# A grouped 3x3 convolution with a residual: where the input waits for its sum, and where the products are added

## The chip, the cores and the metric

The kernel runs on one core of one Trainium2 chip. The metric is the device time of one execution in microseconds. The three runs of the kernel before took 999.61, 989.73 and 990.78 us, median 990.78. The profile is of a further execution, which has its own time.

In what follows PE is the matrix engine, PEld its weight loads, DVE the vector engine, ACT the scalar engine, POOL the general engine (GpSimd), and SP the engine that issues most of the transfers. L494 is line 494 of the kernel before. Where a helper records the operation, its line is shown.

## What is computed

Input x is 160 images of 128 channels by 32 x 32, in float32 (512 KB an image). U holds five sets of weights for a 3x3 convolution from 128 to 128 channels. Image 5b + n uses set n.

```python
s1 = (max(U) - min(U)) / 3;  v1 = s1 * floor(U / s1)
s2 = s1 / 5;                 v2 = s2 * floor((U - v1) / s2)
w = v1 + v2                               # the weights, quantised twice
g = groupnorm(x, 32 groups, eps=1e-5)     # 4 channels x 1024 points a group
out = x + conv3x3(g, w[set of the image], padding 1)
```

So each output image is the input image plus a product: the input is needed twice, to be normalised and to be added.

## The kernel before

**Order of the work.** `Main.run` walks the images set by set: image i is number i % 32 of set i // 32. The order on every engine is the order in which this program issues instructions; it is written by hand (a manual schedule), and every engine and every transfer queue takes its instructions in that order. One iteration of the loop issues the matmuls of image i and, for other images, what must run beside them: PE products of i + 1 (`sums_of_pairs`), DVE low part of i + 2, ACT high part of i + 3, POOL and DVE combinations of i + 4 (L674, L704 on POOL; L686, L693 on DVE), and the statistics of images up to 14 ahead (`STAT_LEAD`), which on ACT are L241 and L248. Three of five images are "combined": differences and sums of neighbouring columns are taken on the image before it is normalised, which needs fewer matmuls (L839) than the other images do (L784 as well). For other images POOL normalises (L710).

**Input buffers.** Images are loaded in pairs ("chunks", 1 MB) by SP, L494, into one of 12 buffers named xt. A load is issued when the loop is within `LOAD_LEAD` = 20 images of the chunk (chunks 0 to 5 before the loop, so chunk 6 is images 12 and 13). The tile framework makes it wait until what was in the buffer has been used and stored.

**Leaving PSUM.** An image's product is finished in a pair of PSUM banks (eo). In the next iteration `residual` copies it on ACT to one of 3 sum buffers (L922), and `accumulate` lets POOL issue a transfer that adds the sum buffer onto the image in its xt buffer, in SBUF (L945, 512 KB). Fifteen images are added "by hand", by DVE, from PSUM onto the image (L937, L939, L929): the first three, the last four (`LAST`), and every sixteenth (i % 16 == 7) after image 30.

**Stores.** At the end of iteration i `store(i - 2)` lets SP store a whole chunk, L950, if i - 2 is its second image. The last four images are stored singly (L941, L932). The store waits for both accumulations.

**SP's queue.** Loads, stores and the weights' loads (L487, one per set, for sets 1 to 4 in the loop: at iteration 2, and for set n + 2 at the last but one image of set n) stand in one queue. Each iteration ends with these two steps:

```python
            while loaded * NB < min(self.imgs, i + self.LOAD_LEAD):
                self.load(loaded)
                loaded += 1
            self.store(i - 2)
```

**Weights.** A set's quantisation is a list of single steps (`Later`), taken a few per iteration on DVE, with some on ACT (L134). It begins at image 1 of the set before (at image 4 for set 1); its first step is ACT's L134, which reads the loaded weights (tile u).

Of the kernel before, what the change touches and what calls it, by code (L numbers as in the profile page):

```python
# [11 lines left out]
ALU = mybir.AluOpType  # L12
# [9 lines left out]
NB = 2  # L22
LAST = 4
# [13 lines left out]
class Later:  # L37


    def __init__(self, steps=(), pace=0.0):  # L40
        self.steps = iter(steps)
        self.pace, self.due = pace, 0.0
        self.scalar = False
# [19 lines left out]
    def finish(self):  # L63
        run(self.steps)
# [256 lines left out]
def general_path(tc, keep, steps, x, u, out):  # L321
# [8 lines left out]
    with tc.If(far > 0), ExitStack() as ctx:  # L330
# [9 lines left out]
        for n in range(N_SETS):  # L340
            un = one.tile([P, C, TAPS], F32, tag="u", name=f"g_u{n}")
            nc.sync.dma_start(un, uv[n])
            wn = one.tile([P, C, TAPS], F32, tag="w", name=f"g_w{n}")
            k1, k2 = run(steps.quantise(one, un, f"g{n}", F32))
            nc.vector.tensor_scalar_mul(wn, k1, steps.s1)
            nc.vector.scalar_tensor_tensor(wn, k2, steps.s2, wn, ALU.mult, ALU.add)
# [38 lines left out]
class Main:  # L385
# [22 lines left out]


    STAT_LEAD = 14  # L410
    LOAD_LEAD = 20
    STEADY = 7
    BY_VECTOR = (8, 10, 11, 14, 19, 24, 29, 34)
    FIFTHS = 30
# [10 lines left out]
    def __init__(self, tc, ctx, keep, x, u, out):  # L425
        self.tc = tc
        nc = self.nc = tc.nc
        self.imgs, C, self.H, self.W = x.shape
        P = self.P = nc.NUM_PARTITIONS
        assert C == P and self.H * self.W == 1024  # L430
        self.per_set = self.imgs // N_SETS
        self.xv = x.rearrange("(b n) c h w -> n c b (h w)", n=N_SETS)
        self.ov = out.rearrange("(b n) c h w -> n c b (h w)", n=N_SETS)
        self.uv = u.rearrange("n (o i k) -> n o i k", o=C, k=TAPS)

        def pool(name, bufs, **kw):
            return ctx.enter_context(tc.tile_pool(name=name, bufs=bufs, **kw))

        self.const = pool("const", 1)
        self.qpool = pool("quant", 1)  # L440
        self.wpool = pool("weights", 2)
        self.upool = pool("u", 1)
        self.xpool = pool("x", 12)
        self.zpool = pool("z", 2)
        self.parts = pool("parts", 4)
        self.rows = pool("rows", 4)
        self.wide = pool("wide", 2)
        self.wide_parts = pool("wide_parts", 3)
        self.evac = pool("evac", 2)
        self.sums = pool("sums", 3)  # L450
        self.unread = pool("unread", 1)
        self.small = pool("small", 3)
        self.ps_eo = pool("ps_eo", 2, space=PSUM)
        ps_m = pool("ps_m", 1, space=PSUM)
        ps_small = pool("ps_small", 1, space=PSUM)
        self.steps = Steps(nc, keep)

        self.m1a, self.m1b, self.m2_ps = (
            ps_m.tile([P, self.H // 2, self.W], F32, tag=name, name=name)
            for name in ("m1a", "m1b", "m2")  # L460
        )
        self.pair = [self.m1a, self.m2_ps]

        small = ps_small.tile([P, 512], F32, tag="small", name="small")
        self.pt, self.pg = small[:, : ROW * P].rearrange("p (k o) -> p k o", k=ROW), small[:, ROW * P :]
        self.chunks, self.z, self.hi, self.v, self.eo, self.m2 = {}, {}, {}, {}, {}, {}
        self.sum = {}
        self.tables, self.wts, self.across = {}, {}, {}
        self.columns = []

        cuts = [0, 2, 4, 8, 12, 16, 20, *range(24, self.imgs + 1, 8)]
        self.groups = [range(a, b) for a, b in zip(cuts, cuts[1:])]
        self.group_of = {i: k for k, g in enumerate(self.groups) for i in g}
        self.stats = {}
# [117 lines left out]
    def keep_sums(self, n, col):  # L592
        wt = self.wts[n, col]
        run(self.both_sums(
            self.nc.gpsimd, wt[:, self.SUM], wt[:, self.DIFF], *(wt[:, k] for k in range(ROW))
        ))
# [317 lines left out]
    def residual(self, i):  # L914

        nc = self.nc
        eo = self.eo.pop(i)
        del self.hi[i]
        n, b = self.place(i)
        if not self.by_hand(i):  # L920
            self.sum[i] = self.sums.tile([self.P, 1024], F32, tag="sum", name=f"sum{i}")
            nc.scalar.copy(self.as_banks(i, self.sum[i]), self.flat(i, eo))  # L922
            return
        xj = self.image(i)
        if i == self.imgs - 1:
            image, banks = self.as_banks(i, xj), self.flat(i, eo)
            for a, quarters in ((0, (slice(0, 512),)), (1, (slice(0, 256), slice(256, 512)))):
                for h, q in enumerate(quarters):
                    nc.vector.tensor_add(image[:, a, q], banks[:, a, q], image[:, a, q])  # L929
                    if a == 1:  # L930
                        half = slice(h * 512, h * 512 + 512)
                        nc.sync.dma_start(self.ov[n, :, b, half], xj[:, half])  # L932
            return
        image = self.as_banks(i, xj)
        if eo is self.pair:
            for a in range(2):
                nc.vector.tensor_add(image[:, a], self.bank(eo, a), image[:, a])  # L937
        else:
            nc.vector.tensor_add(image, self.flat(i, eo), image)  # L939
        if i >= self.imgs - LAST:  # L940
            nc.sync.dma_start(self.ov[n, :, b], xj)  # L941

    def accumulate(self, i):
        if i in self.sum:
            self.nc.gpsimd.dma_start(self.image(i), self.sum.pop(i), accum_op=ALU.add)  # L945

    def store(self, i):
        if 0 <= i < self.imgs - LAST and i % NB == NB - 1:
            n, b = self.place(i)
            self.nc.sync.dma_start(  # L950
                self.ov[n, :, b - NB + 1 : b + 1, :], self.chunks[i // NB]
            )

    def run(self):
        nc, P = self.nc, self.P
# [125 lines left out]
        run(self.combinations(3))  # L1081
        self.steps.choose()
        ready, middle, scaled, measured, loaded = [], [], [], self.EARLY, 6
        later, turned = Later(), []
        for i in range(self.imgs):
            n, b = self.place(i)
# [135 lines left out]
            for k in to_measure:  # L1222
                group = self.group_of[k]
                if k + 1 == self.groups[group].stop:
                    ready.append(self.stats[group])
            while loaded * NB < min(self.imgs, i + self.LOAD_LEAD):
                self.load(loaded)
                loaded += 1
            self.store(i - 2)
        self.residual(self.imgs - 1)  # L1230


# [46 lines left out]
```

## Time and profile before

| | |
|---|---|
| median of 3 runs | 990.78 us (989.73 to 999.61) |
| the profiled execution: its time | 1001.85 us |
| the profiled execution: span in the trace | 1000.1 us |
| mean granted PE clock | 0.988 |
| moved by transfers | 250.05 MB, 250 GB/s |
| read from HBM, written to HBM | 89.19 MB, 83.89 MB |
| loads of a chunk (78 x 1024 KB) | median 7.3 us from issue to landing |
| stores of a chunk (78 x 1024 KB) | median 11.1 us |
| accumulations (145 x 512 KB) | median 8.1 us |

How to read it: a busy time is the sum over the engine's instructions; a line such as "ACT junk L241 <- DMA xt<-in_x_dram: 28.7, 15, 7.6" says that ACT stood idle before the instructions of L241 that write junk, until transfers from the input into xt had landed, for 28.7 us in all, 15 times, 7.6 us at the longest. The waits of SP's queue (SPq) are told apart from those of the computing engines, since a queue may stand without anything being late. In the DMA lines q1 is the queue of SP's transfers, q0 that of POOL's; packets, MB, and the time of the packets as a share of 16 transfer engines. Of the packets those under 512 bytes (5136 in all) are completions; a data packet of an image is 4096 bytes, one row of one partition, so an image is 128 packets, 8 on each engine.

### The profile page before, as it was taken

Reading aid. Unit: us, or ns where it says so; the run is one execution under the profiler, and the core shown is the slowest. Engines: PE = TensorE matmul, PEld = TensorE weight load, DVE = VectorE, ACT = ScalarE, POOL = GpSimd, SP = SyncE. Lnnn points to the kernel's source line nnn. Section 1 sums busy time; section 2 is a strip of 40 time slices with the busy share of each in tenths; the row PEclk is TensorE's granted clock in tenths of the full one; section 3 lists DMA queues with packets and bytes.
Section 4 is the critical chain, followed back from the end, with each engine's and each line's share of the span. In section 5 each row is a group of like instructions: output and inputs, shape, how many; then the busy total and the mean of one; then the engine's idle time right before and its main releaser. Section 6 shows DMA issues by size and latency. Waiting matters only on the chain. (4 is left out here: it accounts for less than half of the span.)

```text
span 1000.1 us, 13146 instructions
## 1 busy us (share of the span) xinstructions
PE 937.4 (94%) x4444; PEld 435.7 (44%) x4444; DVE 917.8 (92%) x1290; ACT 851.9 (85%) x1160; POOL 455.7 (46%) x466
## 2 busy tenths in 40 slices
PE   2999999999999999969999999799999999999996
PEld 1444444444444444424444444344444444444443
DVE  7999999999999999959999999599999978889995
ACT  5789998999999998859889999689988979888551
POOL 4354346445434444514354436244444555555640
PEclk9999999999999999979999999899999999999999
DMA  9738899999999998999999989998999999999765
GB/s 361 285 106 234 222 254 249 250 259 283 264 244 257 258 270 240 258 251 273 280 250 261 259 213 263 285 249 225 285 237 259 276 250 251 243 258 301 179 168 190
DMA packets 66268, 250.05 MB, mean 250 GB/s; under 512 B 5136, under 2 KB 5136, under 8 KB 66192
## 3 DMA queue, kind: packets, MB, share of 16 engines
q1 hardware_dynamic: 45312, 173.09, 51.6%
q0 software_dynamic: 20880, 76.03, 39.2%
q8 instruction: 37, 0.61, 0.2%
q14 instruction: 39, 0.32, 0.1%
HBM read 89.19 MB, written 83.89 MB: 173 GB/s over the span
## 5 line engine op out<-in xcount | busy, mean ns | idle before, releaser
L784 PE MATMUL eo<-hi,wt 128*128 128x496 f16 (+3 forms) x1206 | 319.9, 375 | 1.5 <-ACT wt L566 0.9
L839 PEld LDWEIGHTS <-wt 128*128 128x128 f16 x1884 | 183.9, 99 | 225.2 <-DVE rows L769 12.6
L740 DVE SCALAR_TENSOR_TENSOR vl<-v,rstd,vh 128x2048 f16<-128x2048 f32 x92 | 218.7, 2377 | 2.3 <-ACT vh L734 2.2
L839 PE MATMUL eo<-vh,wt 128*128 128x512 f16 x552 | 207.8, 377 | 0.5 <-DVE eo L898 0.4
L839 PE MATMUL eo<-vl,wt 128*128 128x512 f16 x552 | 207.5, 376 | 0.0
L734 ACT ACTIVATE vh<-v,rstd 128x2048 f16<-128x2048 f32 x92 | 184.1, 2001 | 20.3 <-DVE v L693 20.0
L674 POOL TENSOR_SCALAR v<-xt,ngm 128x64 f32<-128x64 f32 x92 | 79.5, 864 | 238.7 <-issue 100.3
L784 PEld LDWEIGHTS <-wt 128*128 128x128 f16 x1278 | 124.2, 99 | 145.7 <-DVE eo L898 4.0
L241 ACT ACTIVATE junk<-xt 128x1024 uint8<-128x1024 f32 x152 | 160.5, 1056 | 31.5 <-DMA xt<-in_x_dram 28.7
L839 PEld LDWEIGHTS <-across 128*128 128x128 f16 x1104 | 108.7, 98 | 152.6 <-issue 31.1
L248 ACT ACTIVATE junk<-xt,mv 128x1024 uint8<-128x1024 f32 x152 | 174.4, 1147 | 0.1
L922 ACT COPY sum<-eo 128x1024 f32<-128x1024 f32 x145 | 151.6, 1046 | 23.4 <-PE eo L839 21.9
L710 POOL TENSOR_SCALAR z<-xt,ngm,rstd 128x1024 f32<-128x1024 f32 x50 | 89.9, 1798 | 174.4 <-DVE rows L768 63.1
L839 PE MATMUL eo<-rows,wt 128*128 128x496 f16 (+1 forms) x390 | 148.1, 380 | 0.0
L945 POOL DMA_DIRECT2D xt<-sum x145 | 126.8, 874 | 17.8 <-ACT sum L922 15.0
L839 PE MATMUL m<-vh,across 128*128 128x496 f16 (+1 forms) x276 | 104.8, 380 | 11.7 <-ACT m L887 11.7
L839 PE MATMUL m<-vl,across 128*128 128x496 f16 (+1 forms) x276 | 104.8, 380 | 10.2 <-DVE vl L740 10.1
L887 ACT ACTIVATE m<-m 128x512 f32<-128x512 f32 x157 | 93.8, 597 | 20.6 <-PE m L839 16.6
L686 DVE TENSOR_TENSOR v<-xt 128x960 f32<-128x960 f32 x92 | 106.6, 1159 | 0.0
L704 POOL TENSOR_TENSOR v<-xt 128x512 f32<-128x512 f32 x92 | 97.3, 1057 | 0.0
L747 DVE TENSOR_TENSOR lo<-z,hi 128x1024 f16<-128x1024 f32 x68 | 83.1, 1222 | 0.0
L896 DVE SCALAR_TENSOR_TENSOR eo<-m1b,m 128x512 f32<-128x512 f32 x79 | 54.9, 695 | 18.7 <-ACT m L887 16.1
(146 smaller groups left out, 1182.4 us busy)
## 6 DMA issues: line engine op xcount, KB each, us to landing
xt<-in_x_dram SPq DMA_DIRECT2D x78, 1024.0 KB, 7.3
out_dram<-xt SPq DMA_DIRECT2D x78, 1024.0 KB, 11.1
xt<-sum POOLq DMA_DIRECT2D x145, 512.0 KB, 8.1
u<-in_L_conv_U_dram SPq DMA_DIRECT2D x4, 576.0 KB, 14.3
xt<-in_x_dram SPq DMA_DIRECT2D x4, 512.0 KB, 9.6
range<-in_L_conv_U_dram SPq DMA_DIRECT2D x3, 576.0 KB, 7.7
out_dram<-xt SPq DMA_DIRECT2D x3, 512.0 KB, 2.7
u<-in_L_conv_U_dram SPq DMA_DIRECT2D x2, 288.0 KB, 3.1
```

Of the source, the lines that this page charges most:

```text
L241: self.nc.scalar.activation(junk, image, ACTF.Copy, scale=-1.0 / image.shape[1], accum_out=self.mv[:, j, 0:1],)
L248: self.nc.scalar.activation(junk, image, ACTF.Square, bias=self.mv[:, j, 0:1], accum_out=self.mv[:, j, 1:2],)
L686: nc.vector.tensor_tensor(self.view(v, 1, (511, 2), (half, H), (1, half - 1)), self.view(x, 1, (1, 2), (W, H), (2, half - 1)), self.view(x ...
L704: ins = nc.gpsimd.tensor_sub(self.v[i][:, 1536:], odd, even)
L710: ins = nc.gpsimd.tensor_scalar(z, self.image(i), st.ngm[:, j], st.rstd[:, j], ALU.add, ALU.mult)
L734: self.nc.scalar.mul(vh, self.v[i], st.rstd[:, j])
L740: yield self.nc.vector.scalar_tensor_tensor(vl, self.v[i], st.rstd[:, j], self.hi[i], ALU.mult, ALU.subtract)
L784: nc.tensor.matmul(self.bank(target, a)[:, first:end, c0:c1], self.wts[n, col][:, k, :], tile[:, s0 : s0 + 2 * (end - first) - 1 : 2, c0 + ...
L839: self.nc.tensor.matmul(out, weights, moving, start=start and j == 0, stop=False, skip_group_check=True)
L887: self.nc.scalar.mul(m2, self.m2_ps, 0.5)
L922: nc.scalar.copy(self.as_banks(i, self.sum[i]), self.flat(i, eo))
L945: self.nc.gpsimd.dma_start(self.image(i), self.sum.pop(i), accum_op=ALU.add)
```

## The change

A chunk is stored to the output unchanged, as soon as it has been loaded: it is put on a list when its load is issued, and taken from the list, one per iteration, four iterations later or after (`store_input`). The product of an image is then added onto the output in DRAM, not onto the image in SBUF, by the same kind of transfer from POOL; it waits for the store of the image's input (`self.stored`). Images that are added by hand are stored singly, after DVE has added the product, and their chunk's other image is then stored singly too. A load into a used buffer is no longer issued by a fixed lead but when its chunk's images have been read (`consumed`): at image i - 2, or, for an image that is added by hand, at i + 2. `LOAD_LEAD`, 18, governs the first 12 chunks alone. Image 2, the first that is added by hand, is now stored from `residual` at once. Line numbers after L411 move: by 1 at first, by 17 to 23 from `accumulate` on.

```diff
-    LOAD_LEAD = 20
+    LOAD_LEAD = 18
+    CHUNKS = 12
...
-        if i >= self.imgs - LAST:
-            nc.sync.dma_start(self.ov[n, :, b], xj)
+        self.store(i)
 
     def accumulate(self, i):
+
         if i in self.sum:
-            self.nc.gpsimd.dma_start(self.image(i), self.sum.pop(i), accum_op=ALU.add)
+            n, b = self.place(i)
+            added = self.nc.gpsimd.dma_start(
+                self.ov[n, :, b], self.sum.pop(i), accum_op=ALU.add
+            )
+            self.after(added, self.stored[i].ins)
 
     def store(self, i):
-        if 0 <= i < self.imgs - LAST and i % NB == NB - 1:
-            n, b = self.place(i)
-            self.nc.sync.dma_start(
-                self.ov[n, :, b - NB + 1 : b + 1, :], self.chunks[i // NB]
-            )
+
+        n, b = self.place(i)
+        return self.nc.sync.dma_start(self.ov[n, :, b], self.image(i))
+
+    def store_input(self, c):
+
+        images = [i for i in range(c * NB, c * NB + NB) if not self.by_hand(i)]
+        if len(images) == NB:
+            n, b = self.place(images[0])
+            stored = self.nc.sync.dma_start(self.ov[n, :, b : b + NB, :], self.chunks[c])
+            self.stored.update((i, stored) for i in images)
+            return
+        self.stored.update((i, self.store(i)) for i in images)
+
+    def consumed(self, c):
+
+        return max(i + 2 if self.by_hand(i) else i - 2 for i in range(c * NB, c * NB + NB))
...
         ready, middle, scaled, measured, loaded = [], [], [], self.EARLY, 6
+        due = [(c, c) for c in range(1, loaded)]
...
-            while loaded * NB < min(self.imgs, i + self.LOAD_LEAD):
+            while loaded * NB < self.imgs and (
+                loaded * NB < i + self.LOAD_LEAD if loaded < self.CHUNKS
+                else i >= self.consumed(loaded - self.CHUNKS)
+            ):
                 self.load(loaded)
+                due.append((i + 4, loaded))
                 loaded += 1
-            self.store(i - 2)
+            if due and due[0][0] <= i:
+                self.store_input(due.pop(0)[1])
         self.residual(self.imgs - 1)
```

More of the change, by code (lines that the diff above doesn't have):

```diff
@@ L442, in __init__ @@
         self.upool = pool("u", 1)
-        self.xpool = pool("x", 12)
+        self.xpool = pool("x", self.CHUNKS)
         self.zpool = pool("z", 2)
@@ L466, in __init__ @@
         self.chunks, self.z, self.hi, self.v, self.eo, self.m2 = {}, {}, {}, {}, {}, {}
-        self.sum = {}
+        self.sum, self.stored = {}, {}
         self.tables, self.wts, self.across = {}, {}, {}
```

## The prediction, made before the changed kernel had run

> **What bounds the kernel now.** I read the page first (engines, slices, queues), then the waits of all engines and of SP's queue, the timelines of SP and ACT around the largest stall, the windows of 25 us, and the DMA view of two windows. The page:
>
> ```profile
> span 1000.1 us, 13146 instructions
> PE 937.4 (94%) x4444; PEld 435.7 (44%) x4444; DVE 917.8 (92%) x1290; ACT 851.9 (85%) x1160; POOL 455.7 (46%) x466
> DMA  9738899999999998999999989998999999999765
> q1 hardware_dynamic: 45312, 173.09, 51.6%
> q0 software_dynamic: 20880, 76.03, 39.2%
> ```
>
> Three things are nearly full at once: PE, DVE, and the 16 DMA engines, at 51.6 + 39.2 = 91% over the span and 9 tenths in nearly every slice. q1 holds loads and stores, q0 the accumulating transfers: 44% of q1's bytes in 76% of its time. The waits, of ACT, then of SP's queue:
>
> ```profile
> ACT junk L241 <- DMA xt<-in_x_dram: 28.7, 15, 7.6
> ACT nnn L134 <- DMA u<-in_L_conv_U_dram: 21.0, 2, 12.0
> ```
>
> ```profile
> SPq L494 <- DMA out_dram<-xt: 702.4, 67, 14.9
> SPq L950 <- DMA xt<-sum: 109.1, 16, 16.1
> ```
>
> SP spends 702 us inside a load's wait: the buffer is free only when the store of its last content has left, and that store waits for two accumulations. While SP stands, all behind it stands. Two timelines show what it costs, SP's and then ACT's:
>
> ```profile
> 411.89 0.42 SPq L950 DMA_DIRECT2D out_dram<-xt  x1
> 425.62 0.37 SPq L494 DMA_DIRECT2D xt<-in_x_dram  x1
> 426.08 0.44 SPq L950 DMA_DIRECT2D out_dram<-xt  x1
> 426.61 0.42 SPq L487 DMA_DIRECT2D u<-in_L_conv_U_dram  x1
> ```
>
> ```profile
> 440.97 0.80 ACT L134 ACTIVATE nnn<-u,s1r 128x384 int16<-128x384 f32 x1 [12.03 <-DMA u<-in_L_conv_U_dram]
> ```
>
> The weights' load stood behind a load that stood behind a store for 13.7 us; it went out at 426.61, ACT wanted it at 428.9 and got it at 440.97. The windows price this and the late stretch (columns: width, PE, PEld, DVE, ACT, POOL busy, clock, DMA share, GB/s):
>
> ```profile
> 400.00:425.00 25.00, 24.75 (x118) 11.34 (x116) 23.15 (x29) 21.90 (x29) 13.95 (x13) 1.00 1.00 257
> 425.00:450.00 25.00, 15.85 (x64) 6.87 (x63) 13.76 (x21) 12.94 (x20) 3.33 (x4) 0.80 0.89 251
> 450.00:475.00 25.00, 25.00 (x121) 11.60 (x121) 24.42 (x35) 24.57 (x34) 11.91 (x13) 1.00 0.99 274
> 625.00:650.00 25.00, 19.78 (x88) 8.82 (x86) 14.94 (x26) 16.29 (x24) 6.97 (x8) 0.86 0.97 284
> 800.00:825.00 25.00, 23.03 (x110) 10.70 (x109) 19.25 (x19) 19.98 (x27) 13.26 (x12) 1.00 0.95 250
> ```
>
> Elsewhere PE and DVE are both at 24 to 25 of 25. From 787 to 898 the chain that ended last is a row of stores, one behind the other. The DMA view of 8 to 24 us (loads alone), then of 100 to 420 us:
>
> ```profile
> q1 hardware_dynamic: 1723, 6.59, 102.3%
> ```
>
> ```profile
> q1 hardware_dynamic: 13897, 53.64, 51.3%
> q0 software_dynamic: 7544, 27.50, 44.2%
> ```
>
> A packet of 4096 bytes costs an engine 1.023 x 16 x 16 us / 1576 = 166 ns where loads are alone (1723 less 147 small ones); in the mix a copy costs 0.513 x 16 x 320 / 13096 = 200 ns and an accumulation 0.442 x 16 x 320 / 6714 = 337 ns, about twice an unhindered copy: it reads two operands.
>
> **The change, part by part.**
>
> *Store early, load without the store's wait.* A chunk's store now needs only its load, so the 702 and 109 us of SP's waiting go. A load into a used buffer still waits for its old store, but that was issued long before (from chunk 21 on, four iterations after its load), and for the engines' last reads. It goes out at iteration 2c-1 for images 2c+24 and 2c+25, 25 images ahead, where it was at most 20. Its first reader comes 14 images ahead, so some 11 iterations of slack stand where there were 6 less SP's delay. The mean pace is (974.9 - 69.8) / 152 = 5.95 us per image, from the first and last accumulation (images 3 to 155). By-hand images (every 16th) hold their chunk 4 iterations longer; their loads keep 7, or 41 us.
>
> What goes: (a) the weights' waits, 12.0 + 8.9 = 20.9 us. The other two such loads were not waited for. The load is now issued some 4 iterations (23 us) before its reader; the median landing was 14.3. (b) From 800 to 925 us PE idles 5.6 us in five windows, with 1.8 us of half clock: 7. ACT's other waits on loads outside that stretch lie beside a busy DVE: 0. Behind the stalls the next limit is late at once: DVE at 24.5 of 25 in sets 0 to 3, PE after that. Sum: 28 us. All of PE's idle time between 75 and 975 us (33) and the lost clock (10: half speed for about 20 us) bound it from above: 43; from below 0, if the DMA engines, not SP, are what is late (second case below).
>
> *The front of SP's queue.* Image 2's store, which did not exist as a separate one, now stands ahead of the loads of images 12 to 17 and waits for DVE's L937, which ended at 54.04. Those loads went out between 15 and 24 us; now at about 54.5. Image 12 lands after 0.5 + 1 MB at 412 GB/s (6.59 MB in 16 us) plus 2 us, at 60; ACT read it at 59.4 and stood 2.3 us for PE at 62.9: 0. Behind it are 3 loads, 2 half stores, a load and set 1's weights: 6.1 MB, 15 us, so 72 against ACT's 72.4: between 0 and 4, I take 1.
>
> *Stores of the first 20 chunks.* They go out one per iteration, twice the pace, when the DMA slices at 50 to 125 us have 0.17 to 0.65 of their time free; backlog is covered by the 11 iterations. More issues by SP: 14, about 0.4 us each, on a queue that is now idle: 0.
>
> *POOL's wait for the early store.* Chunk 5's store is the tightest: behind 5 MB of burst loads from 86 us, at about 228 GB/s beside accumulations, it lands at 112 and image 10 adds at about 122. 0. If it is late, what stands behind on POOL is z or the outer columns of the image 4 ahead, then DVE's L686.
>
> *The accumulation itself.* Count, bytes and POOL's issue (869 ns) stay; the second operand and the result move to DRAM. No row shows such a transfer. From below, the present 337 ns: a load (read from HBM) and a copy in the other direction share one queue and one price. From above 2 x 200 = 400 ns, two mixed copies; with the issues' medians of 11.1 us for a store against 7.3 for a load, 337 x 1.5 = 505 at the extreme. I take 337, the row of the same operation. If landings grow, ACT's L922 waits: three sum buffers give some 16 us, and the median landing is 8.1, the longest 12.1.
>
> The Trainium skill, DMA: Bandwidth & Descriptors, Anatomy of one DMA, speaks against this: the receipt of the last write dominates a transfer's fixed 2 us, and is longest when the target is HBM. By that each accumulation lands later; with 3 buffers it changes nothing in the sum unless the delay passes about 8 us. HBM Reference, Specifications, gives 358 GB/s as a core's share; HBM traffic after is 173 + 2 x 76 = 325 MB, 908 us by that and 789 us by the 412 GB/s read here, so neither binds.
>
> *Sum.* The profiled execution took 1001.85 us: 1001.85 - 28 + 1 = 975. The median of the runs, 990.78, is 11 lower. If those runs simply had less of these stalls, 975 stands; if they were quicker throughout, 964. I take 970.
>
> **Rivals.**
>
> *The DMA engines stay the limit (no change).* From the landing of the last load (about 906) to the end took 94 us before, and must again. Until that load q1 must move, from 54 us on, 148 loads and 156 stores of 8 packets per engine, q0 129 accumulations (to about image 138), and 8 us of weights: at mixed prices 304 x 8 x 0.200 + 129 x 8 x 0.337 + 8 = 842 us. 54 + 842 + 94 = 990, about the median. For it: shares of 0.99 in the windows. Against: at the unhindered 166 ns it is 54 + 759 + 94 = 907, and nothing binds; the DMA now has a full queue where it had SP's gaps.
>
> *Accumulating in DRAM costs more (slower).* Place: q0, all images. Each 10 ns more is 129 x 8 x 0.010 = 10 us once the engines are full. At 400 ns: 990 + 65 = 1055. It decides (1% slower than 1001.85, 1012) from 358 ns at mixed copy prices, from 440 at unhindered ones. For it: DMA has no room; reads of HBM come between writes of HBM. Against: read and write copies cost alike here, and the accumulation's price is just that of two reads.
>
> *A new stall at the front only.* Set 1's weights or image 12 late, 4 to 8 us: 975 to 980. It does not decide the sign.
>
> **How the numbers follow.** About 1% is what a measurement can tell from no change. Stalls gone: 0.50, front stall included, 970, own range 957 to 981. DMA still the limit: 0.17, 981 to 1001. Dearer accumulation: 0.33, 1001 to some 1100, half of it below 1035. So faster 0.50, same 0.17, slower 0.33. Low 955: most of the 43 us bound. High 1035: beyond it lie 0.16 of the third case, and little below 955.
>
> **What would show it.** SP's wait of L494 for out_dram falls from 702 us to under 100; ACT's L134 no longer waits for u; window 425:450 has PE at 24 or more; stores move ahead, and DMA slices after 900 us fall to 5 tenths. The price step is right if q0's share stays near 39% of the span (337 ns each); over 42% at an unchanged span it is wrong, and ACT's L922 or L241 would wait for DMA. I am wrong if PE's idle time grows in windows where DMA is at 1.0.

## The result, and the profile after

The kernel after took 986.12 us (median of 20 runs, 984.95 to 987.55). Beside it the kernel before took 999.0 (20 runs, 985.46 to 1009.21); the ratio is 0.9917, interval 0.9892 to 0.9941, faster by 0.8%. (The ratio leaves out the runs of the kernel before that lie over 1.5% above its fastest, so it is nearer to 1 than the two medians are.) The forecast was 970, range 955 to 1035: the sign held and the time lies inside the range, but the gain is 0.8% where 2.1% was forecast (970 against 990.78). The profiled execution took 985.5 us, against 1001.85 before: 16 us less where the sum said 27. From the page after (written to HBM is higher by 76.02 MB, the accumulations, which wrote to SBUF before):

```profile
span 983.8 us, 13047 instructions
PE 931.5 (95%) x4444; PEld 434.3 (44%) x4444; DVE 915.7 (93%) x1290; ACT 853.2 (87%) x1160; POOL 457.8 (47%) x466
DMA  9079999999989997999799989989997999766653
q1 hardware_dynamic: 45472, 173.09, 45.9%
q0 software_dynamic: 20880, 76.03, 42.6%
HBM read 89.19 MB, written 159.91 MB: 253 GB/s over the span
```

The waits of ACT, then of SP's queue:

```profile
ACT nnn L134 <- DMA u<-in_L_conv_U_dram: 13.2, 2, 11.9
ACT junk L241 <- DMA xt<-in_x_dram: 10.3, 3, 7.6
```

```profile
SPq L955 <- DVE xt L940: 327.1, 12, 90.1
SPq L495 <- DVE v L694: 147.9, 16, 12.7
SPq L962 <- DMA xt<-in_x_dram: 110.7, 21, 11.1
SPq L495 <- POOL z L711: 102.8, 14, 11.2
...
SPq L495 <- DMA out_dram<-xt: 23.6, 11, 6.3
```

SP's loads wait 24 us for old stores, where it was 702. SP's queue is not idle for that: all rows of this view add up to 794 us, against 903 before. It now stands for DVE to finish images that are added by hand (L955), for the last reads of a buffer (L495), and for loads to land (L962). ACT's wait for loaded images fell from 28.7 to 10.3 us, of which 9.4 stand before 60 us in both kernels. One long wait for weights is left, 11.9 us, and it is not one of the two that stood before: it belongs to set 2. The timelines of SP and of ACT show it:

```profile
222.83 0.53 SPq L495 DMA_DIRECT2D xt<-in_x_dram  x1
233.22 0.37 SPq L962 DMA_DIRECT2D out_dram<-xt  x1
233.64 1.05 SPq L488 DMA_DIRECT2D u<-in_L_conv_U_dram  x1
```

```profile
256.66 0.80 ACT L134 ACTIVATE nnn<-u,s1r 128x384 int16<-128x384 f32 x1 [11.94 <-DMA u<-in_L_conv_U_dram]
```

SP stood from 223 to 233 at an early store (L962), which waits until the chunk that it stores, issued at 203.71, has landed; the weights' load was behind it. It went out at 233.64, ACT wanted it at 244.72, and it was used at 256.66. The windows (columns as before: width, PE, PEld, DVE, ACT, POOL busy, clock, DMA share, GB/s):

```profile
225.00:250.00 25.00, 25.00 (x120) 11.52 (x118) 20.23 (x22) 19.53 (x26) 13.66 (x11) 1.00 1.05 305
250.00:275.00 25.00, 17.19 (x77) 7.72 (x76) 16.80 (x29) 18.28 (x26) 8.52 (x9) 0.86 1.03 372
...
425.00:450.00 25.00, 25.00 (x122) 11.89 (x121) 22.52 (x33) 23.84 (x33) 11.32 (x11) 1.00 1.04 330
...
625.00:650.00 25.00, 25.00 (x123) 11.81 (x121) 23.66 (x38) 24.05 (x35) 10.87 (x12) 1.00 1.04 327
...
800.00:825.00 25.00, 25.00 (x122) 11.80 (x121) 23.10 (x32) 24.27 (x33) 12.61 (x10) 1.00 1.05 325
```

The holes at 425, 625 and 800 are filled. A new one stands at 250, where PE was full in the kernel before:

```profile
250.00:275.00 25.00, 25.00 (x121) 11.66 (x119) 24.52 (x35) 23.96 (x36) 12.32 (x14) 1.00 0.98 263
```

After the change PE idles 7.8 us there and runs at a clock of 0.86, which is 0.14 x 25 = 3.5 us more, 11.3 together. Why that load was slow is in the DMA view of 75 to 275 us (last column: median us from issue to landing):

```profile
q1 hardware_dynamic: 12807, 49.32, 62.0%
q0 software_dynamic: 4603, 16.78, 42.0%
...
out_dram<-xt SPq DMA_DIRECT2D x24, 1024.0 KB, 28.0
xt<-in_x_dram SPq DMA_DIRECT2D x18, 1024.0 KB, 28.2
...
u<-in_L_conv_U_dram SPq DMA_DIRECT2D x1, 576.0 KB, 23.0
```

Stores and loads take 28 us to land there: q1 holds a backlog that the early stores make (one chunk per iteration until the first 20 have caught up), and the weights pass through all of it. The share of the DMA engines is 1.03 to 1.05 in every window of 25 us from 75 to 275. The prices from these lines, as the prediction worked them: a copy 0.620 x 16 x 200 / (49.32e6 / 4096) = 165 ns, an accumulation 0.420 x 16 x 200 / (16.78e6 / 4096) = 328 ns. (The two shares add up to 104%, as loads alone gave 102.3%: packets overlap a little on an engine, so these are times of packets, not parts of an engine's time.) Over the whole execution, from the q1 and q0 lines of the two pages, a copy takes 171 ns (195 before) and an accumulation 361 (338 before). At the end, from 850 to 975 us, accumulations are almost alone:

```profile
q0 software_dynamic: 2736, 9.96, 52.6%
q1 hardware_dynamic: 691, 2.57, 5.4%
...
out_dram<-sum POOLq DMA_DIRECT2D x19, 512.0 KB, 5.4
```

There one costs 0.526 x 16 x 125 / (9.96e6 / 4096) = 433 ns, but it lands in 5.4 us, where the median of the earlier stretches is 8.4 to 8.9.

### The profile page after: what moved, and what is told of

The parts are those of the page before. It is cut to its first block, busy times and chain, and to the rows that moved or that the text cites. A ratio compares the mean times of both kernels' runs of the same rounds, so it can differ in the third digit from the quotient of the medians.

```text
span 983.8 us, 13047 instructions
## 1 busy us (share of the span) xinstructions
PE 931.5 (95%) x4444; PEld 434.3 (44%) x4444; DVE 915.7 (93%) x1290; ACT 853.2 (87%) x1160; POOL 457.8 (47%) x466
## 3 DMA queue, kind: packets, MB, share of 16 engines
q0 software_dynamic: 20880, 76.03, 42.6%
HBM read 89.19 MB, written 159.91 MB: 253 GB/s over the span
## 5 line engine op out<-in xcount | busy, mean ns | idle before, releaser
L675 POOL TENSOR_SCALAR v<-xt,ngm 128x64 f32<-128x64 f32 x92 | 84.7, 921 | 218.6 <-issue 63.5
L923 ACT COPY sum<-eo 128x1024 f32<-128x1024 f32 x145 | 151.6, 1045 | 28.7 <-PE eo L840 28.2
L241 ACT ACTIVATE junk<-xt 128x1024 uint8<-128x1024 f32 x152 | 160.4, 1055 | 13.5 <-DMA xt<-in_x_dram 10.3
L947 POOL DMA_DIRECT2D out_dram<-sum x145 | 126.8, 875 | 9.1 <-ACT sum L923 5.2
L705 POOL TENSOR_TENSOR v<-xt 128x512 f32<-128x512 f32 x92 | 95.2, 1035 | 0.0
L286 POOL TENSOR_TENSOR rstd<-ve,mhalf 128x8 f32<-128x8 f32 (+2 forms) x24 | 44.5, 1853 | 60.5 <-DVE rows L770 20.2
```

Source lines behind the costliest of these rows:

```text
L241: self.nc.scalar.activation(junk, image, ACTF.Copy, scale=-1.0 / image.shape[1], accum_out=self.mv[:, j, 0:1],)
L705: ins = nc.gpsimd.tensor_sub(self.v[i][:, 1536:], odd, even)
L947: added = self.nc.gpsimd.dma_start(self.ov[n, :, b], self.sum.pop(i), accum_op=ALU.add)
```

## The experiments

The theory: the change does what the sum says, 975, less one thing, set 2's weights, delayed by the backlog of early stores; without that the time is 975. The rivals: the DMA engines are the limit after all; the accumulation in DRAM is what costs; another wait stands right behind the weights'. The kernels below are the kernel after with the edit shown, unless said otherwise. Times are medians; the kernel before had medians of 997.6 to 1001.6 beside them. The kernel after was not run again beside them, so its 986.12 is compared across sessions.

**Weights through ACT's queue.** The weights' loads alone leave SP's queue.

```diff
-        self.nc.sync.dma_start(self.us[n], self.uv[n])
+        self.nc.scalar.dma_start(self.us[n], self.uv[n])
```

> The changed kernel, but the weights' four loads in the loop are issued from ACT's queue, so that they do not stand behind SP's transfers. Theory 1 (set 2's weights came late only because the early stores had filled SP's queue; 11.9 us of ACT's wait): that wait falls under 2 us, the time to 986 - 11 = 975. Theory 2 (the transfer engines, at a share of 1.04 from 75 to 275 us, are the limit, and the wait only shows where): the time stays at 984 to 988, and ACT waits for xt or the sums as long instead.

Measured: 977.91 us (976.81 to 981.41, 10 runs; the profiled execution 980.54). The wait for u is gone, the loads land in 8.8 us at the median. 3 us more than 975, and ACT's waits from 220 to 250 us show a new one:

```profile
ACT junk L241 <- DMA out_dram<-xt: 3.5, 1, 3.5
```

L241 reads an image; it has no business with a store. In ACT's order the issue of the weights' load stands there, and what it waited for was a store that SP had issued. So at least 8 of the 11 us come from the weights' place, and the new route has a small wait of its own.

**Late stores.** The backlog alone is taken away: a chunk's store waits for iteration 2c - 5, so that stores go out at the pace of the loads from the start. The weights stay in SP's queue.

```diff
-                due.append((i + 4, loaded))
+                due.append((max(i + 4, 2 * loaded - 5), loaded))
```

> The changed kernel, but chunk c's input is not stored before iteration 2c - 5, so that stores go out at one per two iterations from the start, as in steady work, and not one per iteration. Theory 1: the median landing of a store between 75 and 275 us falls from 28.0 us to under 16, set 2's weights land within 16 us of their issue, ACT's wait for them falls under 3 us, the time to about 975. Theory 2: 984 or more, since the same bytes have to be moved with less of a head start; a load then waits for its buffer's store again.

Measured: 974.76 us (974.26 to 975.64, 10 runs). The DMA view of 75 to 275 us, then SP's timeline:

```profile
out_dram<-xt SPq DMA_DIRECT2D x17, 1024.0 KB, 15.8
...
u<-in_L_conv_U_dram SPq DMA_DIRECT2D x1, 576.0 KB, 14.2
```

```profile
213.37 0.47 SPq L488 DMA_DIRECT2D u<-in_L_conv_U_dram  x1
```

17 stores fall in the stretch instead of 24. The weights go out 20 us earlier (SP does not stand for landings) and land 9 us sooner; ACT waits 0.2 us. PE in 250 to 275 is at 25.00. The 11 us are the backlog's. SP's loads wait for old stores again, as theory 2 said, and it costs nothing:

```profile
SPq L495 <- DMA out_dram<-xt: 175.2, 32, 13.1
```

**Before, with only the weights moved.** The kernel before, weights' loads through ACT's queue: is the change worth more than that?

> The kernel before, with this edit alone: the weights' loads issued from ACT's queue. If the weights' waits are most of what the kernel before lost (my 20.9 of 28 us): profile 1000 - 20 = 980, runs at 978 to 984, and the whole change is worth some 7 us beyond that. If the row of stores that follow one another is what costs, and the weights' wait only its first sign: 990 or more, with ACT's wait for xt grown.

Measured: 992.85 us (982.66 to 999.18, 10 runs), which is not clearly different from the kernel before (997.62, 974.38 to 1011.97, 31 runs). Both waits for u are gone, but ACT's other wait and SP's are these:

```profile
ACT junk L241 <- DMA xt<-in_x_dram: 49.3, 22, 7.8
```

```profile
SPq L494 <- DMA out_dram<-xt: 706.4, 68, 15.3
```

The images are late in the weights' place: 49.3 us instead of 28.7. The stalls of the kernel before were not the weights' own; the row of stores and loads made them. With the weights on ACT's queue on both sides, the change is worth 992.85 - 977.91 = 15 us.

**Plain writes.** The first experiment, and POOL's transfers write instead of adding (`accum_op` left out): the addition of the input is left out, so the output is the product alone.

> As the first of these kernels (weights from ACT's queue), but POOL's transfers write the product over the stored image and do not add: the addition of the input is left out for all images that are not added by hand. An accumulation's packet of 327 ns should become one of about 160, and q0's share of 42.6% about 21%. Theory 1: no engine was waiting for the transfers any more, the time is that of the first kernel within 3 us. Theory 2: it is at least 10 us lower.

Measured: 975.06 us (974.76 to 977.13, 10 runs). From its page:

```profile
q0 software_dynamic: 20880, 76.03, 19.3%
```

More than half of the accumulations' time is gone, 0.426 x 983.8 - 0.193 x 973.5 = 231 us on each engine, and the time does not go below 975. The accumulation's price is not on the path; the DMA engines' share falls with it, to 0.61 in the window at 250, and that does not help either.

**Late stores and weights through ACT's queue.** Is anything left of the weights?

> Late stores (not before iteration 2c - 5) and the weights' loads from ACT's queue together. If the weights' wait was the only thing that the early stores cost, there is nothing left to win: 974 to 976, as with late stores alone. If SP's queue still costs something in sets 3 and 4: 970 or less.

Measured: 975.07 us (974.58 to 977.36, 12 runs). Nothing.

**Weights' load issued two images earlier.** In "after" `b == self.per_set - 2` becomes `- 4`: the backlog stays, the lead grows.

> The changed kernel, with the weights' loads of sets 2 to 4 put two iterations earlier in SP's queue (after image 28 of a set, not 30), still behind the early stores. If what came late was the issue, since SP stood for landings of loads (it went out at 233.6 us): the issue moves 11 us or more ahead and ACT's wait of 11.9 us falls under 2, time 975 to 978. If the landing in the filled queue (23 us) is what counts: the wait stays over 5 us, time 981 or more.

Measured: 981.22 us (979.99 to 982.34, 10 runs). SP, then ACT:

```profile
223.09 0.53 SPq L488 DMA_DIRECT2D u<-in_L_conv_U_dram  x1
```

```profile
252.11 0.81 ACT L134 ACTIVATE nnn<-u,s1r 128x384 int16<-128x384 f32 x1 [6.69 <-DMA u<-in_L_conv_U_dram]
```

Issued 10.5 us earlier, it was there only 4.5 us earlier: its landing took 29.0 us instead of 23.0. The wait fell by 5.3 us and the time by 4.9, so this wait is paid one for one; and the full queue counts, not the moment of issue alone.

**More to move, weights in SP's queue.** Late stores, and each whole chunk is stored once more to a spare tensor in DRAM: half of it (35.7 MB, about 91 us on each engine at 166 ns per 4096 bytes), then all of it (71.3 MB, 181 us).

```diff
+        self.spare = nc.dram_tensor("spare", [N_SETS, P, self.per_set, 1024], F32, kind="Internal").ap()
...
+            self.nc.sync.dma_start(self.spare[n, :, b : b + NB, :512], self.chunks[c][:, :, :512])
```

> Late stores, and beside each store of a whole chunk (68 of them) a second one of its first half rows to a spare tensor in DRAM that nothing reads: 16 packets of 2048 bytes per engine and chunk, 84 ns each where they are alone, so 91 us more work for each transfer engine. If copies cost what they cost unhindered (166 ns), the sum of the prediction was 907 and this one 907 + 91 = 998. If the engines were the limit already at mixed prices (200 ns), all of it is added: 975 + 91 = 1066.

> As the one before, but the second store is of the whole chunk: 16 packets of 4096 bytes, 166 ns each, 68 times, 181 us more. Unhindered prices: 907 + 181 = 1088. Engines the limit already: 975 + 181 = 1156. If the transfers overlap better than either sum says: less than 1060.

Measured: 988.52 us and 1027.13 us (2 runs each): below every sum of the two expectations (998 and 1066, 1088 and 1156), as only the last line of the second allowed. ACT's waits with half, then with all of it:

```profile
ACT nnn L134 <- DMA u<-in_L_conv_U_dram: 15.8, 3, 13.4
```

```profile
ACT nnn L134 <- DMA u<-in_L_conv_U_dram: 43.2, 4, 20.7
ACT sum L924 <- DMA out_dram<-sum: 12.1, 3, 8.1
```

Taken alone the first would say that the engines are full. But the waits that grew are again the weights', behind SP's queue: two causes were mixed, and the next runs part them.

**The same two, weights through ACT's queue.**

> Late stores, half a chunk more stored to spare DRAM per chunk (91 us more for each transfer engine), and the weights' loads from ACT's queue. If a full transfer queue costs only through the weights, the one load without a lead: back to 975 to 978, though the engines move 286 MB and not 250. If the images' loads or the sums are late as well: 985 or more.

> As the one before with a whole chunk more (181 us more per transfer engine, 322 MB in all). In the run without the queue's change ACT waited 43 us for weights and 12 us for accumulations to land, of 52 us added. If only the weights count: 1027 - 43 = 984, with 12 us of ACT's wait for the sums left in it. If the transfer engines are the limit by now: within 10 us of 1027, and the wait moves to ACT's copies or to the images.

Measured: 987.81 us (8 runs) and 1020.77 us (2 runs). The first should have fallen to 975 and did not, but the weights landed in 8.3 us and the wait was another:

```profile
ACT junk L241 <- DMA spare<-xt: 10.5, 1, 10.5
```

This is the wait of the first experiment in larger: ACT's issue of a weights' load stood 10.5 us for a store of SP's. PE's hole there (225 to 250 us: 9.2 us idle, 5.0 us of lost clock) is as large as the whole loss of 13 us, so the run says nothing against the engines. With all of it, late images and late sum buffers stand at the head of ACT's waits:

```profile
ACT junk L241 <- DMA xt<-in_x_dram: 28.4, 5, 10.9
ACT sum L924 <- DMA out_dram<-sum: 18.8, 8, 7.5
```

There, at 321 MB in 1020 us and 97% of the engines' time, transfers are 42% of the chain that ended last. That the engines are the limit there is likely but not shown: SP's loads stand for stores again (328 us for the output, 245 for the spare tensor), and no run parts this from the engines.

**Weights through POOL's queue.** POOL's transfers go by q0, apart from SP's. "After" with `self.nc.gpsimd.dma_start` in L488, the early stores as they were; then the same edit on the late stores with half a chunk more.

> The changed kernel with early stores as they are, but the weights' loads issued from POOL's queue, which holds only the accumulations. With ACT's queue 3.5 us were lost before the issue, in a wait for one of SP's stores. If the weights behind the stores are all that the early stores cost: 974 to 976, as with late stores. If the engines' full queue itself costs: 980 or more.

> Late stores, half a chunk more stored to spare DRAM per chunk (91 us more for each transfer engine), weights from POOL's queue. With ACT's queue 10.5 us were lost in a wait for a spare store before the issue. If 91 us of transfer work are free as long as nothing without a lead stands in the queue: 974 to 977. If not: 985 or more, as in the two runs before.

Measured: 975.11 us (974.64 to 975.36, 4 runs), ratio 0.9756 (0.9715 to 0.9796), and 974.83 us (974.58 to 975.67, 4 runs). The DMA view of 75 to 275 us of the first, then the page of the second:

```profile
out_dram<-xt SPq DMA_DIRECT2D x23, 1024.0 KB, 28.2
...
u<-in_L_conv_U_dram POOLq DMA_DIRECT2D x1, 576.0 KB, 11.9
```

```profile
span 973.3 us, 13134 instructions
...
DMA  9079999999999999999999999999999999998653
...
q1 hardware_dynamic: 63392, 206.39, 54.8%
q0 software_dynamic: 21456, 78.39, 40.9%
```

The first leaves the backlog whole (stores still take 28.2 us) and takes only the weights out of it: 975. POOL issued set 2's load at 225.66, 8 us before SP had, and it landed 11 us sooner. With the DMA engines as busy as before, PE's hole at 250 is closed:

```profile
250.00:275.00 25.00, 25.00 (x122) 11.79 (x120) 24.34 (x36) 24.39 (x35) 12.36 (x13) 1.00 1.04 341
```

So the late weights are the single cause of the 11 us. The second moves 35.7 MB more, has DMA at 9 tenths in every slice from the fourth to the 36th (73 to 876 us), 95.7% over the span, and costs nothing, though SP's loads stand 417 us for stores. Weights by POOL's queue, like the late stores, are 11 us under the kernel after, and 23 to 24 us under the median of the kernel before; the quickest runs of that kernel (974.2 us) are as quick.

## Why the prediction was right or wrong

**Right: SP's row of stores.** Its waits for old stores went from 702 to 24 us and the windows at 425, 625 and 800 filled, as promised; PE's idle time from 800 to 925 us is 1.0 us, from 5.6. Late stores show that SP's standing is no cost by itself (175 us for old stores, and 975 all the same): it costs where something behind it has too little lead.

**Right: the sum, as a floor.** The sum said 975 for the profiled execution. Six kernels that take the weights' wait away by different routes and leave the accumulation, or leave it out, or add 36 MB, lie at 974.8 to 977.9, five of them at 975.

**Wrong: "Stores of the first 20 chunks ... backlog is covered by the 11 iterations", 0.** This is the step that failed. The covering holds for images: after 60 us ACT waited 0.9 us for them. It does not hold for set 2's weights, which stand in the same queue at the time of the backlog without the images' lead. The prediction looked for free time of the DMA engines at 50 to 125 us; in the kernel before, the windows of 25 us after that have only 0.02 to 0.07 of it until 225, so the backlog could not drain there. After the change the share stays at 1.03 or more until 275, and set 2's load is issued at 233.64. The term was 11 us (11.3 in the window; 986.1 - 975.1 by the experiment).

**Wrong for one load: "issued some 4 iterations (23 us) before its reader".** Set 2's had 244.72 - 233.64 = 11.1 us. Sets 3 and 4 went out at 405.67 and 593.99 and were read at 439.17 and 624.17 without a wait, over 30 us later. The lead was worked out as if SP's queue stood idle, "on a queue that is now idle"; it waited 794 us in all, 110.7 of them for the landings of chunks that it was to store (L962 above). The kernel before had delayed sets 3 and 4 because SP stood for stores; this one delayed set 2 because SP stood for loads, and its queue was full. The median landing of 14.3 us was the other half: in the backlog it was 23.0. That "the other two such loads were not waited for" was true, but the kernel before had little to spare for set 2 (SP, then ACT):

```profile
227.16 0.47 SPq L487 DMA_DIRECT2D u<-in_L_conv_U_dram  x1
```

```profile
244.24 0.81 ACT L134 ACTIVATE nnn<-u,s1r 128x384 int16<-128x384 f32 x1
```

The load took 15.4 us to land, so it was there 1.7 us before its reader.

**Wrong: the step from 975 to 970.** It took half of the 11 us by which the median of three runs lay below the profiled execution. Of 20 runs the median is 999.0, close to the profiled 1001.85. The floor does not move with it.

**Near enough: the accumulation at 337 ns.** It is 328 ns in the backlog and 361 over the whole execution, 7% more than the 338 before, and q0's share passed the 42% that was named as the sign of an error (42.6%). Of the 27 us more that this makes on each engine, the last 125 us, at 433 ns, hold about half. No one waited for it: ACT's wait for the sum buffers did not appear, the median landing grew from 8.1 to 8.7 us, and plain writes give the same 975, so the dearer-accumulation rival was bound to a limit that is not there.

**The rival "DMA engines stay the limit", 990.** The time, 986, falls close to it, and that is chance: half a chunk more each time, with the weights out of the way, costs nothing. The sign "PE's idle time grows in windows where DMA is at 1.0" came true at 250 us (7.8 us at 1.03), but for another reason: with the weights on POOL's queue the same window has DMA at 1.04 and PE full. The rival's price of 200 ns for a copy was that of the mix before; after, a copy takes 165 to 171 ns, close to the rival's own unhindered price, at which "nothing binds".

**The front.** ACT's two waits for images before 60 us, 9.4 us in all, stand in the kernel before as well. Set 1's weights were waited for 1.3 us, where the sum had 1; PE's busy time from 50 to 100 us is the same in both kernels, so this can't be told from 0. SP issues 10 stores more (91 of whole and half chunks, from 81), where the prediction counted 14; at 0.4 us each that decides nothing.

A rule of the Trainium skill on the same point, in DMA: Bandwidth & Descriptors, Issuing engines are not separate DMA queues: all transfers run on the same 16 engines, so issuing from another engine only saves the time of issuing. Here that would be four issues of some 0.6 us. The measured effect of the other queue is 986.12 - 975.11 = 11 us: the engines are shared, but within SP's queue the load stood behind what was issued before it (issued at 233.64 and 23.0 us to landing from SP's queue, 225.66 and 11.9 from POOL's, in the same backlog). The measurement decides.

What stays open: why runs of the kernel before differ so much (974 to 1012 us over all sessions, where the kernels of 975 keep within 3). Its best runs lie at the same floor, so it may be that its stalls vary; no trace here shows one of those runs.

## What to carry to other kernels

When a change fills a queue, look for the load with the least lead in that queue, not at the mean one: work out for each whether its issue time, behind all that the queue waits for, plus its landing in the full queue, still meets its reader. A rare load that something waits for (a set's weights) belongs in a queue apart from the stream, or the stream's burst is to be thinned out. And a time that agrees with a rival's number is no proof of the rival: the DMA engines looked full at 9 tenths in most slices and had room for 36 MB more.

## What the runs showed of the hardware that was not expected

- A copy's packet of 4096 bytes took 195 ns in the kernel before, where the accumulations write to SBUF, and 171 in the kernel after, where they write to DRAM (whole executions; 166 where loads are alone). No run changes that target alone, so the cause is not shown. Accumulations took 338 and 361 ns; almost alone, into DRAM, 433 ns.
- A transfer issued by ACT can be held by one that SP issued: its issue waited 3.5 and 10.5 us for stores from xt, with which it shares no data. In the trace the two name the same completion semaphore: in the run with 3.5 us, number 105 stands at SP's store issued at 201.85 us and at ACT's load, which waits for it and is issued at 227.42; in the run with 10.5 us it is 105 again (215.17 and 234.35). A run in which only this sharing is taken away was not made.
- The second operand of the accumulation, read from DRAM after the change, isn't counted in "HBM read": it is 89.19 MB in both kernels, and also with plain writes, which read no second operand.
